# Layer 3 of a recurrent network with experts: two pairs of state space groups written amid the blocks of experts

## The chip, the core and the metric

The kernel runs on one core of one Trainium2 chip. A core has five engines with a queue of instructions each: TensorE (PE, with its weight loads PEld), VectorE (DVE), ScalarE (ACT), GpSimd (POOL) and SyncE (SP). The metric is the device time of one execution in microseconds, as the median of several runs.

## What is computed

The program is four layers over an input of 2 sequences of 1024 tokens with 128 features. Each layer has the form

```
xn = layernorm(x)
s = sequence_mixer(xn)          # layer 3: two state space models, forward and backward
g = silu(mixture_of_experts(xn))
x = x + s * g
```

Only layer 3, the last, matters here. Its mixer runs one state space model over the first 64 features and one, backwards in time, over the other 64; both end in a common projection. Cut to one direction:

```
zxbcdt = u @ in_w.T                       # split into z, x, B, C, dt
x, B, C = silu(conv(x, B, C))             # 4 taps along time
h = exp(dt * A) * h + dt * outer(x, B)    # the state, step by step
y = (h @ C + D * x) * silu(z)
out = rmsnorm(y) @ outp_w.T
```

Its mixture sends each token to 2 of 16 experts and adds a shared expert:

```
hidden = silu(x @ gate[e]) * (x @ up[e])
out = sum over the token's two experts of weight * (hidden @ down[e]) + shared(x)
```

## The kernel before

**State space.** The 2048 tokens are 16 tiles of 128, in four groups (g = 0 to 3) of four tiles. The class `StateSpace` (L413) handles a unit of one direction, one sequence b and one half n of it, that is one group of tokens. `pairs` in `layer3` (L1659) lists four pairs of units, forward and backward together: pair 0 is the first half of sequence 0 in each direction's own sense, pair 1 its second half, pairs 2 and 3 the same for sequence 1. The backward direction starts at the end of its sequence, so pair 3 ends the groups 2 and 3. A pair has two steps:

- `stacked` (L452) makes convolved inputs: the products `px` (L287, the helper that records every matmul) and Silu into `uxs` (L473), and the gates `pz` into `usz` (L483).
- `unit` (L535) does the rest. `uda` (L556) and the product `pd` and Exp into `uE` (L559) make decays inside a tile of 128 tokens; `uwide` (L562) and `pe` make `ueA` (L568); transposes `pt` (L578) make `uxdt` (L580), `uxst` (L581) and `uBt` (L583); `pcb` and `ucb` (L589) are multiplied into `uE` (L592); `pst` and `ustate` (L612) carry the state from tile to tile; `py` (L627) and `pi` (L635 to L637) make the output `uy`; its squares `ut` (L638) are summed by `pss` into `ur` (L299 to L301, with a square root on ScalarE between two VectorE instructions), and `pyo` is scaled by `ur` and added into `xn` (L1736).

`unit` takes `busy`: when it is true, `uda`, `uwide`, `uxst`, the multiplication into `uE` and the two last steps of `uy` are VectorE's, else GpSimd's. Pairs 0, 1 and 2 have it true, pair 3 false. `together` (L654) steps its generators in turn, so that a pair's directions, and the `stacked` of the next pair, are written interleaved. All of `StateSpace` takes its PSUM banks from a pool of four, the experts from another of four.

**Experts.** `Dispatch` (L1129) sorts the tokens by expert into 47 lists of 128 rows. They are worked in twelve blocks of four (three in the last). A block gathers its rows by indirect DMAs on GpSimd's queue (`load`, L1231, `xb`, two buffers), loads weights on SP's queue (`weights`, L1237, `tw`, three buffers), and on TensorE does transposes `pxb` (L1772), the product `pgb`, transposes `phb` (L1784) and the product `pob`; ScalarE has the Silu `sgb` (L1779), VectorE the product `hb` (L1781), and copies `xbT`, `hbT`, `yb` go to VectorE and ScalarE in turn (`Kern.copy`, L278 to L284). Each list's result is scattered into `ys` by an indirect DMA on GpSimd's queue (`store`, L1241). The shared expert (`pgt`, `put`, `hT` L1804, `psh`) is written behind the blocks into `acc`.

**The end.** For each group `fetch` (L1246) loads its slots `yt` from `ys` on SP's queue (L1252, four buffers), which waits for every scatter, and VectorE adds them to `acc` (L409). Then come a Silu (L1813), the product with `xn`, which holds the state space's result (L1814), the sum with x (L1815) and the output's DMA (L1816).

**Order.** The source is written in this order: `stacked` for pairs 0 and 1, the unit pair 0, all blocks of experts, the shared expert, pairs 1, 2 and 3, the fetches. Instructions don't run in the written order: in the build (L1864, `schedule_with_timeline_sim=True`) a scheduler that models time places them in each engine's queue, and the written order is its priority. On the chip each queue then runs strictly in the built order. Layer 2's attention alone has an order written by hand.

Of the kernel before, what the change touches and what calls it, by code (L numbers as in the profile page):

```python
# [653 lines left out]
def together(*parts):  # L654

    live = list(parts)
    while live:
        live = [p for p in live if next(p, p) is not p]


def grp(a, g):
    return a[:, g * G : (g + 1) * G, :]
# [996 lines left out]
def layer3(K, x, xn, xT, w, inp, out):  # L1659
    nc, tc, c = K.nc, K.tc, K.c  # L1660
    four = [P, G, P]
    with ExitStack() as es:
# [84 lines left out]
        space = StateSpace(K, pa, sa, parts)  # L1747
        pairs = [[(m, b, n) for m in parts] for b in range(NB) for n in range(TPB // G)]
# [6 lines left out]
        def load_rows(n0):  # L1755
            loaded[n0] = pf.tile(four, F32, name="xb", bufs=2)
            for n in range(n0, min(n0 + 4, d.n)):
                d.load(loaded[n0][:, n - n0, :], n)

        load_rows(0)  # L1760
        for n0 in range(0, d.n, 4):
            part = range(n0, min(n0 + 4, d.n))
            m = len(part)
            if n0 + 4 < d.n:
                load_rows(n0 + 4)
            xb = loaded.pop(n0)
            tw = pf.tile([P, 4, 256], F32, name="tw", bufs=3)
            for n in part:
                d.weights(tw[:, n - n0, :], n, inp["rows"])
            pt = sf.tile(four, F32, name="pxb", tag="ps")[:, :m, :]  # L1770
            for r in range(m):
                nc.tensor.transpose(pt[:, r, :], xb[:, r, :], c["ident"])  # L1772
            xbT = pf.tile(four, F32, name="xbT", bufs=2)[:, :m, :]
            K.copy(xbT, pt)
            pg = sf.tile(four, F32, name="pgb", tag="ps")[:, :m, :]
            for r in range(m):
                K.mm(pg[:, r, :], xbT[:, r, :], tw[:, r, :P])
            sg = pf.tile([P, 4, 64], F32, name="sgb", bufs=2)[:, :m, :]
            nc.scalar.activation(sg, pg[:, :, :64], AF.Silu)  # L1779
            hb = pf.tile([P, 4, 64], F32, name="hb", bufs=2)[:, :m, :]  # L1780
            nc.vector.tensor_mul(hb, sg, pg[:, :, 64:])  # L1781
            pt = sf.tile([64, 4, P], F32, name="phb", tag="ps")[:, :m, :]
            for r in range(m):
                nc.tensor.transpose(pt[:, r, :], hb[:, r, :], c["ident"])  # L1784
            hbT = pf.tile([64, 4, P], F32, name="hbT", bufs=2)[:, :m, :]
            K.copy(hbT, pt)
            po = sf.tile(four, F32, name="pob", tag="ps")[:, :m, :]
            for r in range(m):
                K.mm(po[:, r, :], hbT[:, r, :], tw[:64, r, P:])
            yb = pf.tile(four, F32, name="yb", bufs=2)[:, :m, :]  # L1790
            K.copy(yb, po)
            for r, n in enumerate(part):
                d.store(yb[:, r, :], n)
        acc = pa.tile([P, NT, P], F32, name="acc", tag="acc")
        for g in range(NG):
# [10 lines left out]
            for j in range(G):  # L1806
                K.mm(po[:, j, :], hT[:, j * P : (j + 1) * P], w["sd"])
            K.copy(grp(acc, g), po)
        for n, p in enumerate(pairs[1:]):
            together(*(space.unit(*u, busy=n < 2) for u in p), *(space.stacked(q) for q in pairs[n + 2 : n + 3]))  # L1810
        for g in range(NG):
            d.fetch(pe, acc, g, w12)
            nc.scalar.activation(grp(acc, g), grp(acc, g), AF.Silu)  # L1813
# [5 lines left out]
def build(tc, io, packs):  # L1819
    nc = tc.nc  # L1820
    with ExitStack() as ctx:
        pool = ctx.enter_context(tc.tile_pool(name="const", bufs=1))
        x = pool.tile([P, NT, P], F32, name="x")
        src = io["x"].rearrange("b (t p) d -> p (b t) d", p=P)
        for g in range(NG):
            nc.sync.dma_start(grp(x, g), src[:, g * G : (g + 1) * G, :])
        xn = pool.tile([P, NT, P], F32, name="xn")
        xT = pool.tile([P, T], F32, name="xT")

        def load(into, n, by=nc.scalar):  # L1830
            t = into.tile([P, packs[n].n], F32, name="w_" + n)
            by.dma_start(t, io[n])
            return View(t, packs[n])

        K = Kern(tc, load(pool, "c"))
        dram = ctx.enter_context(tc.tile_pool(name="lists", bufs=1, space=DRAM))
        lists = {n: dram.tile([rows, P], F32, name=n) for n, rows in (("xs", T), ("ys", 2 * T))}
        views = {}
        with tc.tile_pool(name="const0", bufs=1) as pool0:
            w0 = load(pool0, "l0")  # L1840
            e0 = load(pool0, "e0")
            layer0(K, x, xn, xT, w0, e0)
        later = ctx.enter_context(tc.tile_pool(name="const3", bufs=1))
        views["l3"] = load(later, "l3")
        pair = lists["xs"], lists["ys"]
        with tc.tile_pool(name="const2", bufs=1) as pool0:
            views.update((n, load(pool0, n)) for n in ("l1", "l2"))
            layer1(K, x, xn, xT, views["l1"], {"rows": io["rows1"], "lists": pair, **{n: io[n] for n in ("sw1", "sw3", "sw2")}})
            layer2(K, x, xn, xT, views["l2"], {"rows": io["rows2"], "lists": pair})
        layer3(K, x, xn, xT, views["l3"], {"load": lambda pool: load(pool, "x3", nc.sync), "rows": io["rows3"], "lists": pair}, io["out"].rearrange("b (t p) d -> p (b t) d", p=P))  # L1850
# [17 lines left out]
```

## Time and profile before

| what | us |
|---|---|
| runs | 1360.89, 1365.46, 1372.87 |
| median | 1365.46 |
| the profiled execution, its own time | 1410.96 |
| its span from the first to the last instruction | 1409.1 |
| TensorE busy in the span | 1153.0 |
| VectorE busy | 877.0 |
| ScalarE busy | 623.3 |
| GpSimd busy | 430.2 |

The profiled execution took 45.5 us longer than the median of the runs; its granted TensorE clock was 0.883 on the mean. Positions in the profile are in us from the span's start. Layer 3 begins near 1117, its first gather of rows is issued at 1188.6. In a line of the timeline stand start, duration, engine, source line, operation, out<-in, shape and count, and in brackets the idle time of the engine ahead of it and what ended it. In the chain of waits stand start, duration, engine and what. A float32 matmul shows as two records in the timeline.

### The profile page before, as it was taken

To read this page: it belongs to the slowest core of one execution; us is meant where nothing else is said; L and a number is where in the kernel's file an instruction comes from. 1 tells how busy PE (TensorE), PEld (TensorE's weight loads), DVE (VectorE), ACT (ScalarE), POOL (GpSimd) and SP (SyncE) were. 2 spreads that over 40 slices of the span, in tenths; PEclk is the share of its full clock that TensorE was granted. 3 is DMA by queue.
4 is the path that set the end of the run, shared out by engine and by line. 5 is a ranking of instruction groups with operands and counts; after the bars stand their busy time and mean duration, and the time that the engine had idled before them with its cause. 6 is when DMAs were issued, how large, how long until landed. Compare 5 with 4: busy or idle time off the path is not lost. (4 is left out here: it accounts for less than half of the span.)

```text
span 1409.1 us, 19118 instructions
## 1 busy us (share of the span) xinstructions
PE 1153.0 (82%) x6813; PEld 800.4 (57%) x6813; DVE 877.0 (62%) x2169; ACT 623.3 (44%) x1042; POOL 430.2 (31%) x424
## 2 busy tenths in 40 slices
PE   5599776797997568999998997599998379788885
PEld 2276455785897335444444433377787355657664
DVE  6536336945654776777777635977673577544356
ACT  7656916116322251554556674125522164253351
POOL 0352260036455240000000000156565122556543
PEclk9799986889999876899999898899999768897897
DMA  2000003113343200000000000133345311222311
GB/s 87 0 1 1 0 15 119 46 41 123 119 143 102 60 1 0 1 1 1 1 1 16 8 1 8 75 86 116 120 135 161 104 37 56 66 67 80 53 44 52
DMA packets 49040, 75.71 MB, mean 54 GB/s; under 512 B 7336, under 2 KB 36403, under 8 KB 48689
## 3 DMA queue, kind: packets, MB, share of 16 engines
q1 hardware_dynamic: 39632, 54.30, 12.3%
q0 software_dynamic: 8448, 14.98, 4.7%
q10 hardware_dynamic: 864, 5.21, 1.0%
q8 instruction: 54, 0.88, 0.3%
q14 instruction: 42, 0.34, 0.1%
HBM read 63.95 MB, written 12.85 MB: 55 GB/s over the span
## 5 line engine op out<-in xcount | busy, mean ns | idle before, releaser
L1458 DVE TENSOR_REDUCE mx<-pm 128x1 f32<-128x512 f32 (+3 forms) x304 | 182.0, 656 | 65.3 <-PE pm L287 63.0
L1231 POOL DMA_INDIRECT xb<-xs,dfrom x132 | 134.9, 1022 | 158.3 <-PE pxb L1772 35.4
L1502 ACT ACTIVATE pr<-psc 128x1024 f32<-128x1024 f32 x144 | 139.5, 1021 | 95.1 <-PE psc L287 61.4
L1241 POOL DMA_INDIRECT ys<-yb,dto x132 | 134.5, 1019 | 87.7 <-DVE yb L1119 34.7
L1206 POOL TENSOR_TENSOR dhh<-dhh,w_c 128x1280 fp32r<-128x1280 f32 (+2 forms) x3 | 8.8, 2917 | 476.0 <-DVE dhh L1205 476.0
L287 PE MATMUL pm<-kT,qT 32*128 32x128 f32 (+3 forms) x576 | 118.8, 365 | 16.4 <-DVE mx L1458 12.5
L287 PE MATMUL p<-xbT,tw 128*128 128x256 f32 x368 | 103.0, 396 | 8.4 <-ACT sg L1112 3.0
L287 PEld LDWEIGHTS pm<-kT,qT 32*128 32x128 f32 x576 | 69.1, 203 | 68.9 <-DVE mx L1458 49.1
L1112 ACT ACTIVATE sg<-p,tw 128x256 f32<-128x256 f32 x92 | 41.1, 473 | 102.4 <-PE p L287 86.5
L287 PE MATMUL pat<-pr,va 128*32 128x512 f32 x576 | 82.0, 637 | 0.2 <-ACT pr L1502 0.2
L293 PE MATMUL tp<-w_c,xn 128*128 128x128 f32 x64 | 20.2, 428 | 71.8 <-DVE xn L328 44.0
L287 PEld LDWEIGHTS p<-xbT,tw 128*128 128x128 f32 x368 | 63.8, 196 | 20.3 <-issue 5.8
L1113 DVE SCALAR_TENSOR_TENSOR hh<-p,tw,sg 128x256 f32<-128x256 f32 x92 | 42.6, 478 | 44.2 <-ACT sg L1112 22.9
L287 PE MATMUL psc<-qT,kT 32*128 32x512 f32 x288 | 64.1, 490 | 3.3 <-ACT pr L1502 3.1
L287 PEld LDWEIGHTS po<-tw,hh 128*128 128x128 f32 x368 | 54.2, 192 | 8.7 <-issue 2.2
L293 PEld LDWEIGHTS tp<-w_c,xn 128*128 128x128 f32 x64 | 11.8, 190 | 80.3 <-DVE xn L328 28.1
L287 PE MATMUL po<-tw,hh 128*128 128x128 f32 x368 | 56.2, 276 | 1.0 <-DVE hh L1113 0.7
L287 PE MATMUL psc<-mT,onesR 32*128 32x512 f32 x288 | 53.8, 414 | 0.0
L282 ACT COPY xbT<-pxb 128x256 f32<-128x256 f32 (+3 forms) x39 | 15.6, 400 | 70.8 <-PE pxb L808 35.4
L287 PEld LDWEIGHTS psc<-qT,kT 32*128 32x128 f32 x288 | 30.3, 189 | 16.5 <-ACT pr L1502 14.4
L287 PE MATMUL pd<-uda,w_c 128*128 128x512 f32 x64 | 38.1, 708 | 0.9 <-ACT usz L528 0.9
L287 PE MATMUL pcum<-kv,w_c 128*128 128x512 f32 x64 | 34.2, 635 | 3.4 <-DVE prod L1322 3.1
(528 smaller groups left out, 2824.5 us busy)
## 6 DMA issues: line engine op xcount, KB each, us to landing
tw<-in_rows SPq DMA_DIRECT2D x23, 836.0 KB
tw<-in_rows SPq DMA_DIRECT2D x39, 384.0 KB
yt<-ys SPq DMA_DIRECT2D x24, 256.0 KB
tw<-in_rows SPq DMA_DIRECT2D x47, 128.0 KB
xb<-xs,dfrom POOLq DMA_INDIRECT x132
ys<-yb,dto POOLq DMA_INDIRECT x132
xs<-xn SPq DMA_DIRECT2D x8, 256.0 KB
w_l<-in_l ACTq DMA_DIRECT2D x1, 1890.0 KB
```

The source lines that it names most:

```text
L282: self.nc.scalar.copy(out, in_)
L287: self.nc.tensor.matmul(out, lhsT=lhsT, rhs=rhs, start=start, stop=stop)
L293: self.nc.tensor.transpose(pt[:, j, :], src(g * G + j), self.c["ident"])
L1112: nc.scalar.activation(sg, p1[:, k - k0, :], AF.Silu, bias=t[:, 1536 + k : 1537 + k])
L1113: nc.vector.scalar_tensor_tensor(hh[:, k, :], p2[:, k - k0, :], t[:, 1540 + k : 1541 + k], sg, ALU.add, ALU.mult)
L1206: nc.gpsimd.tensor_mul(h, h.bitcast(F32), c["slot"][:, at].unsqueeze(2).to_broadcast(shape))
L1231: self.K.nc.gpsimd.indirect_dma_start(dst, None, self.xs, bass.IndirectOffsetOnAxis(self.of_token[:, n : n + 1], 0))
L1241: d = self.K.nc.gpsimd.indirect_dma_start(self.ys, bass.IndirectOffsetOnAxis(self.to[:, n : n + 1], 0), src, None, bounds_check=2 * T - 1, ...
L1458: nc.vector.tensor_reduce(mx[:, starts.index(a), g, j : j + k], tile[0][:, : k * m].rearrange("p (j m) -> p j m", m=m), AX.X, ALU.max)
L1502: K.nc.scalar.activation(pr, ps, AF.Exp, scale=scale)
```

## The change

In `layer3` pairs 1 and 2 are written ahead of blocks 5 and 9 (the loop's n0 = 16 and 32), each with the `stacked` of the pair behind it; pair 3 stays behind the shared expert. Which pairs are `busy` stays the same.

```diff
+        def pair(n):
+            together(*(space.unit(*u, busy=n < 3) for u in pairs[n]), *(space.stacked(q) for q in pairs[n + 1 : n + 2]))
+
         load_rows(0)
         for n0 in range(0, d.n, 4):
+            if n0 in (16, 32):
+                pair(n0 // 16)
             part = range(n0, min(n0 + 4, d.n))
...
             K.copy(grp(acc, g), po)
-        for n, p in enumerate(pairs[1:]):
-            together(*(space.unit(*u, busy=n < 2) for u in p), *(space.stacked(q) for q in pairs[n + 2 : n + 3]))
+        pair(3)
         for g in range(NG):
             d.fetch(pe, acc, g, w12)
```

## The prediction

> **What bounds the kernel now.** I read the busy time by stage of layer 3, then the chain that ended last, then the queues of GpSimd and TensorE. Below, "pair k" is the k-th of the four pairs of state space groups (0 to 3), "block k" the k-th of the twelve blocks of experts. The change touches pairs 1, 2 and 3.
>
> ```profile
> core 0: us, PE busy (x) PEld busy (x) DVE busy (x) ACT busy (x) POOL busy (x), PEclk, DMA share, GB/s
> 1231.00:1295.40 64.40, 55.66 (x287) 40.45 (x286) 27.45 (x63) 25.04 (x38) 37.40 (x37) 0.83 0.25 69
> 1295.40:1350.30 54.90, 47.61 (x261) 33.66 (x261) 22.95 (x53) 23.43 (x36) 29.86 (x30) 0.88 0.32 52
> 1350.30:1363.90 13.60, 10.81 (x41) 5.96 (x40) 4.21 (x12) 6.43 (x11) 9.09 (x9) 0.87 0.02 2
> 1363.90:1390.00 26.10, 22.11 (x152) 17.52 (x150) 22.36 (x59) 11.86 (x17) 8.58 (x7) 0.93 0.35 102
> 1390.00:1409.00 19.00, 7.20 (x32) 6.90 (x32) 6.76 (x19) 3.15 (x6) 4.92 (x4) 0.59 0.09 28
> ```
>
> The cuts are the ends of pairs 0, 1 and 2 and of the last scatter. TensorE is 87% busy under pairs 1 and 2 and sets the pace there. So pairs 1 and 2 already run amid the blocks: pair 2's last product (pyo) ends at 1350.3, block 12's product (pob) at 1359.4. The scheduler of the build made that order, though the source writes them behind the blocks. What lies behind the last scatter is pair 3, and the last 19 us are nearly empty.
>
> ```profile
> 1362.89 2.21 DMA ys<-yb,dto
> 1365.26 0.38 SPq L1252
> 1365.69 4.37 DMA yt<-ys
> ...
> 1390.81 2.48 POOL uy L636 x2
> 1393.29 1.23 POOL uy L637
> 1394.54 0.64 ACT ut L638
> 1395.22 3.57 PE pss L287 x16
> 1398.80 1.93 PE pyo L287 x8
> ```
>
> This is the chain: block 12's last scatter, the fetch of all slots that must wait for it, VectorE's sums, then the tail of pair 3 (gates on GpSimd, square, pss, pyo). From the end of the last scatter's issue (1363.9) to the end (1409.1) it is 45.2 us.
>
> ```profile
> 1357.23 0.99 POOL L1241 DMA_INDIRECT ys<-yb,dto  x1 [0.30 <-issue]
> 1358.21 1.08 POOL L556 TENSOR_TENSOR uda<-w_c,vdA 128x512 f32<-128x512 f32 x1
> 1360.27 1.02 POOL L1241 DMA_INDIRECT ys<-yb,dto  x1 [0.98 <-ACT yb L282]
> ...
> 1371.45 2.12 POOL L581 TENSOR_TENSOR uxst<-uxdt,vex 128x512 f32<-128x512 f32 x2 [5.68 <-DVE uxdt L580]
> 1377.44 5.84 POOL L592 TENSOR_TENSOR uE<-uE,ucb 128x512 f32<-128x512 f32 x4 [3.87 <-DVE ucb L589]
> ```
>
> GpSimd issues a gather or scatter every 1.3 us (1.0 and 0.3 between), four per block each way, and does pair 3's elementwise work in the same queue.
>
> **The change part by part.** No operation is added or removed but two ACT table loads; `busy` is true for pairs 1 and 2 and false for 3, as before. Written places only set priorities, so I compared the built orders. They are equal on all engines until block 5 and on SP throughout (no weight load changes its place; block 12's waits for block 9's pob to free its buffer, near 1338, and is first used some 20 us later). Then the state space runs one block ahead of where it ran, and pair 3 is pulled forward. TensorE after pair 2's end, and GpSimd's end, now read:
>
> ```
> PE   pd, phb10, pd x2, pob10, pxb11, pd, pe, pgb11, phb11, pob11, pxb12,
>      pe, pt, pgb12, pt, pcb, phb12, pst x4, pob12, shared ..., py, pi, pss, pyo
> POOL xb12 x3, ys9 x4, uda x2, ys10 x4, uwide, ys11 x4,
>      uxst x2, uE x4, ys12 x3, uy x4
> ```
>
> Before, pair 3's uxst, uE and all its products from the last pd on stood behind block 12's scatters.
>
> *What moves ahead of block 12.* On TensorE one pd (1.0), pe (2.1), pt (2.1), pcb (1.95), four pst (1.2): 8.3 us by the rows behind 1362 in this trace. On GpSimd uxst and uE, 2.1 + 5.8 us. All of it sits on the way to the last scatter, so it is not hidden.
>
> *Delay of the last scatter, D.* Let T0 be the end of block 10's input transposes (pxb), which free block 12's gather. Before, pair 2's second pi ended at 1342.2. One block less now lies ahead of it (0.66 + 1.13 + 0.60 + 1.16 = 3.5), block 9's pob and block 10's pxb follow it (1.8), and TensorE's 15.9 us of waits between 1231 and 1350 (its bracketed idle times in the timeline) shrink a little, since two long ones (before pob and pe) get other work in between; I take 1.5. T0 = 1342.2 - 3.5 + 1.8 - 1.5 = 1339.0. From there the GpSimd queue, in order:
> - gather of block 12, 0.4 + 3.8, then ys9 4 x 1.3: T0 + 9.7 with the gap;
> - uda x2, 2.1: T0 + 11.8. Pair 3's third pd stands behind this on TensorE and waits about 2 us (by durations in order, TensorE is there at T0 + 8.7); behind it wait pob10 and all of block 11;
> - ys10: its product is copied at about T0 + 13.6, so a wait of 1.8, then 5.2: T0 + 18.8; uwide 0.9;
> - ys11: block 11's Silu waits for an exp-to-Silu table load, so yb is ready at about T0 + 21.3; then 5.2: T0 + 26.5;
> - uxst, 2.1: T0 + 28.7. The four pst, and block 12's pob behind them on TensorE, wait for this (2 us);
> - uE x4 at 1.08 (as uxst) to 1.49 (its own median): 4.3 to 6.0, I take 5.0[...]; T0 + 33.7;
> - ys12 3 x 1.3: T0 + 37.5 = 1376.5.
> So D = 1376.5 - 1363.9 = 12.6 us. Lower end: no waits in the queue (33.7) and all 15.9 us of TensorE's waits gone: D near -6. Upper end: below, under the slower rival.
>
> *Tail, S.* Counted from the end of the last scatter's issue, by the rows of before: first yt used at +4.3, the second at +6.3 (1368.2 and 1370.15); twelve adds at 0.3 to +9.9; hT 0.7; copy 0.7; two multiplications and two additions to x 3.4; eight adds 2.2: +16.9. Pair 3's py and pi run under ys12 and its uy right behind (5.0); its squares queue on ACT behind group 0's Silu (to +10.9), pss and pyo 3.6 + 3.7 at the low clock of the old tail: +18.2. But its Sqrt stands on ACT behind group 2's Silu: 16.9 + 0.8 + table 1.3 + 0.4 = +19.4, so this decides. Then eight xn 2.2 and recip 0.2: +21.8; the rest of group 3 with group 2's close 3.8; Silu 0.8; multiply and add 1.4; the output 3.5 as before: +31.3. Tail 31.3 against 45.2: S = 13.9.
>
> Sum: 12.6 - 13.9 = -1.3 us, 1409.1 to 1407.8. The profiled execution took 1410.96, the median of the runs is 1365.46 (a factor of 0.968), so -1.3 there too: about 1364.
>
> [...] First the table loads. Row: ACT_TABLE_LOAD 1.28 us, the activation behind it starting at once (1303.45 + 1.28, then 1304.74). [...] Two loads more and one on the tail's path: by the row +1.3 on the path (in S already)[...]. Second, GpSimd for elementwise work. Rows: uE takes 0.684 us on VectorE and 1.49 on GpSimd. [...] here it is nearer 2.2 times. This speaks against the change: before, these six operations delayed no scatter; now they cost 7.1 us ahead of the last one. [...]
>
> **Rivals.**
> (1) *Traded, my forecast*: scatter later by about as much as the tail shortens; its own range is 1356 to 1372. For it: TensorE at 87% has no room for pair 3 for nothing.
> (2) *GpSimd and the waits don't bind*: most of the 15.9 us of waits are filled and D is 0 or less. Then S remains: -13.9, 1351.5. For it: TensorE was idle 2.8 us of the 13.6 between 1350.3 and 1363.9. Against it: the pulled-forward products need GpSimd results behind scatters.
> (3) *Slower: GpSimd's queue becomes the bound.* Place: uda behind ys9, and uxst behind ys11, each holding TensorE, whose blocked pob holds the next scatter. Price: if each round trip costs the longest wait of GpSimd for TensorE in before (7.0, instead of the 2 I took) that is +10; uE at its largest 1.71 adds 1.8[...], so about +12, and 1377; with a third such trip at ys10 about +17, 1382. It decides once the last scatter is issued later than 1363.9 + 13.9 = 1377.8, only 1.3 us behind my sum, and costs over 1% from 1391.5.
> (4) *It does next to nothing*, since pairs 1 and 2 were amid the blocks already: 1365.5. Against: pair 3 does move.
>
> **Numbers.** About 1% (14 us) is what a measurement can tell from no change. Chances: (1) 0.50; (4) 0.14; (2) 0.18, two thirds of it beyond 1%; (3) 0.18, most of it beyond 1%. Hence faster 0.12, same 0.72, slower 0.16. The range goes from (2) at 1351 to between the two prices of (3), 1379.
>
> **What would show it.** Right: last scatter near 1376; a tail of about 31; uxst and uE directly before block 12's scatters; the 5.3 us hole of TensorE before pss off the chain. Wrong: a last scatter before 1366 (rival 2) or after 1390 (rival 3), or a tail over 38, in which case pair 3's gates, not the fetch, still end last.

## The result, and the profile after

| | median us | lowest to highest | runs |
|---|---|---|---|
| before | 1361.18 | 1355.2 to 1372.87 | 22 |
| after | 1369.96 | 1362.55 to 1374.98 | 22 |

The ratio is 1.0056, with a 95% interval from 1.0041 to 1.0071: 8.8 us more, where the forecast was 1.3 us less. It is a loss of less than 1%, but clear of the noise: the interval is 0.15% to each side, where the prediction took 1% for the least that can be told.

First the busy time by stage of layer 3 in the changed kernel (core 0, span 1368.0 us), cut as in the prediction: pairs 1 and 2, then to the end of the last scatter's issue, then the tail in two pieces. Each row has the window, its length, the busy time and count on TensorE, its weight loads, VectorE, ScalarE and GpSimd, the granted clock and the DMA share.

```profile
core 0: us, PE busy (x) PEld busy (x) DVE busy (x) ACT busy (x) POOL busy (x), PEclk, DMA share, GB/s
1209.00:1258.00 49.00, 45.08 (x263) 33.34 (x262) 25.30 (x57) 23.32 (x34) 32.40 (x31) 0.92 0.30 82
1258.00:1298.70 40.70, 40.54 (x258) 29.73 (x257) 20.62 (x48) 23.91 (x35) 26.44 (x27) 1.00 0.40 69
1298.70:1335.40 36.70, 29.25 (x162) 21.36 (x161) 12.94 (x36) 15.48 (x23) 24.82 (x25) 0.86 0.09 14
1335.40:1349.00 13.60, 7.64 (x48) 5.74 (x48) 10.52 (x23) 3.48 (x6) 4.98 (x4) 0.78 0.50 141
1349.00:1368.00 19.00, 6.37 (x44) 5.15 (x42) 11.93 (x37) 5.31 (x8) 0.00 (x0) 0.77 0.22 65
```

This table must not be set beside the one in the prediction. The chip of that profile is not on record, but its stages are those of a chip on which the kernel takes some 1415 us (the first experiments below give the grounds); this one was taken where it takes 1361. The same rows of the kernel before from a chip of the second kind (run before_third, span 1357.0), for pairs 1 and 2 and the time to the last scatter:

```profile
core 0: us, PE busy (x) PEld busy (x) DVE busy (x) ACT busy (x) POOL busy (x), PEclk, DMA share, GB/s
1208.50:1256.50 48.00, 45.22 (x285) 32.88 (x285) 26.38 (x59) 24.11 (x37) 32.47 (x32) 0.99 0.29 85
1256.50:1299.00 42.50, 41.20 (x261) 30.10 (x260) 23.87 (x56) 23.30 (x36) 33.21 (x33) 1.00 0.40 74
1299.00:1312.40 13.40, 10.61 (x39) 5.67 (x38) 3.54 (x9) 6.29 (x10) 9.03 (x9) 0.87 0.02 3
```

Read it so: in both kernels pairs 1 and 2 take 90 us together (48.00 + 42.50 and 49.00 + 40.70). But before, 13.4 us remain from there to the last scatter, and after 36.7. TensorE is idle for 7.4 of these 36.7 us, and the clock is 0.86.

To compare runs I count from the start of dhh, the last large GpSimd product ahead of layer 3's first gather. "E" is the end of the last scatter's issue, "tail" the rest of the span:

| profile | chip's time of the kernel before | E | tail | stage |
|---|---|---|---|---|
| before, of the prediction | not on record; about 1415 by its stage | 186.7 | 45.2 | 231.9 |
| before_third | 1360 | 148.8 | 44.6 | 193.4 |
| after | 1361 | 171.1 | 32.6 | 203.7 |

So, like for like, the last scatter is 22.3 us later (forecast 12.6) and the tail is 12.0 us shorter (forecast 13.9): 10.3 us longer in these two profiles, 8.8 by the runs.

The GpSimd queue of the changed kernel behind pair 2, from its timeline:

```profile
1303.29 0.98 POOL L1241 DMA_INDIRECT ys<-yb,dto  x1 [0.30 <-issue]
1304.29 2.05 POOL L556 TENSOR_TENSOR uda<-w_c,vdA 128x512 f32<-128x512 f32 x2
1310.42 1.02 POOL L1241 DMA_INDIRECT ys<-yb,dto  x1 [4.09 <-ACT yb L282]
...
1319.87 0.99 POOL L1241 DMA_INDIRECT ys<-yb,dto  x1 [3.94 <-DVE yb L284]
...
1324.68 2.07 POOL L581 TENSOR_TENSOR uxst<-uxdt,vex 128x512 f32<-128x512 f32 x2
1326.69 4.96 POOL L592 TENSOR_TENSOR uE<-uE,ucb 128x512 f32<-128x512 f32 x4
1331.81 1.02 POOL L1241 DMA_INDIRECT ys<-yb,dto  x1 [0.17 <-issue]
```

The order is the forecast one, and uda, uxst and uE take what was put in (2.1, 2.1, 5.0). The two waits in brackets, 4.1 and 3.9 us, are where it runs late. TensorE at the same place, where the four products of pob, two records each, are an x8:

```profile
1305.40 2.08 PE L287 MATMUL pd<-uda,w_c 128*128 128x512 f32 x2 [4.40 <-POOL uda L556]
1307.40 2.07 PE L287 MATMUL pob<-tw,hbT 64*128 64x128 f32 x8
1309.41 1.11 PE L1778 MATMUL pxb<-w_c,xb 128*128 128x128 f32 x4
...
1316.36 0.63 PE L1790 MATMUL phb<-w_c,hb 128*64 128x128 f32 x4 [2.27 <-DVE hb L1787]
```

TensorE waits 4.40 us for uda, and what follows runs at half clock, granted 0.50 from 1305.5 to 1312.2: pob takes 2.07 us where the next one takes 1.16, pxb 1.11 where 0.66 is usual (before_third). Pieces of the chain that ended last, from the last scatter on:

```profile
1334.41 2.08 DMA ys<-yb,dto
1336.65 3.90 DMA yt<-ys
...
1346.37 2.09 PE psh L287 x8
...
1353.77 1.28 ACT L300
1355.06 0.21 ACT ur L300
```

The tail ends by the fetched slots and the table load in front of group 3's Sqrt, no longer by pair 3's gates, as forecast. 32.6 us were measured, 31.3 forecast.

### The profile page after: what moved, and what is told of

Read it like the earlier page. It is cut to its first block, busy times and chain, and to the rows that moved or that the text cites. A ratio compares the mean times of both kernels' runs of the same rounds, so it can differ in the third digit from the quotient of the medians.

```text
span 1368.0 us, 19121 instructions
## 1 busy us (share of the span) xinstructions
PE 1140.1 (83%) x6813; PEld 794.4 (58%) x6813; DVE 876.3 (64%) x2169; ACT 625.0 (46%) x1044; POOL 429.5 (31%) x424
## 3 DMA queue, kind: packets, MB, share of 16 engines
q1 hardware_dynamic: 39632, 54.30, 12.8%
## 5 line engine op out<-in xcount | busy, mean ns | idle before, releaser
L282 ACT COPY xbT<-pxb 128x256 f32<-128x256 f32 (+3 forms) x39 | 15.6, 399 | 66.9 <-PE pxb L808 45.2
## 6 DMA issues: line engine op xcount, KB each, us to landing
w_l<-in_l ACTq DMA_DIRECT2D x1, 1890.0 KB, 11.4
```

The lines of the kernel that those rows point to most:

```text
L282: self.nc.scalar.copy(out, in_)
```

## The experiments

Two explanations stood against each other at the start. **Queue**: the loss is pair 3's uda, uxst and uE between GpSimd's scatters, with TensorE held behind them. **Order**: the loss lies already in pairs 1 and 2, whose shift leaves one more block behind pair 2, whatever pair 3 does. A third came in after the first runs, **chip**: the sum was read off a profile from a chip on which this stage takes another time. In the diffs `decays` puts pair 3's uda and uwide on VectorE, `inside` its uxst and uE.

### Does the profile of before show this kernel, and on which chip?

before_again, before_third and before_fourth are the kernel before, unchanged; after_again and after_third the changed one, unchanged.

before_again, as expected on record:

> The kernel before, unchanged, for a second profile. The first profiled execution of it took 1410.96 us, 50 us over the median of the runs, while that of the changed kernel took 1369.84, its median. If the first was an outlier, this one is near 1361 us, with about 196 us from the last multiplication by the slots (uninterrupted start of the dispatch, 1177.2 in the first profile, 232 us before its end) to the end, and a tail behind the last scatter well under 45 us. If profiling simply slows this kernel, it is near 1410 again.

before_third, as expected on record:

> The kernel before, unchanged, for a profile on the chip of this call. Theory C (chips differ): on a chip where before runs near 1361 us, layer 3 from its last one-hot multiplication (dhh) to the end takes about 195 us, with few waits of an engine that no engine ends; on one near 1415 us about 235 us, as in the two profiles had so far.

before_fourth, as expected on record:

> The kernel before, for a profile from the same chip as the other two. About 193 us from dhh to the end and no idle time of VectorE without a shown releaser if the kernel takes about 1360 us here; 232 to 238 us and more than 20 us of such idle time if it takes about 1416.

Measured: before_again took 1418.51 us, on a chip where the median of before over 59 runs was 1417.62. So it is not profiling that slows it, since all 59 runs there took about as long. My expectation of about 1361 missed; the "near 1410" of the other branch came out, but not for the reason that it gives. before_third took 1358.86 (median there 1360.25), before_fourth 1363.22 (1360.75). The runs fell on five chips: two take about 1360 us, three 1414 to 1418, and no median in between occurred. Of the 59.6 us between the spans of before_again and before_third (1416.6 and 1357.0), 44.3 lie in this stage: 237.7 against 193.4 us. There, on the longer chips, VectorE stands idle in pieces of 1.5 to 5.2 us for which the profile shows no releaser. Three of them, from the timeline of before_again, and TensorE's wait behind the first:

```profile
1246.06 0.42 DVE L1781 TENSOR_TENSOR hb<-sgb,pgb 128x256 f32<-128x256 f32 x1 [4.45 <-issue]
1246.54 0.63 PE L1784 MATMUL phb<-w_c,hb 128*64 128x128 f32 x4 [3.02 <-issue]
...
1329.78 0.29 DVE L608 COPY ustate<-pst 128x128 f32<-128x128 f32 x1 [2.47 <-remote]
...
1341.60 0.75 DVE L627 SCALAR_TENSOR_TENSOR uy<-uxs,w_l,py 128x512 f32<-128x512 f32 x1 [3.80 <-remote]
```

In the stage such pieces of over 1 us make 28.6 us on VectorE in before_again, and none in before_third. In the profile of the prediction they make 25.0, and its stage takes 231.9 us; this is why I count it among the longer chips. TensorE's bracketed waits between the ends of pairs 0 and 2 tell them apart as well: 15.9 us in the profile of the prediction and 16.0 in before_again, but 4.0 in before_third and in before_fourth. What makes the idle pieces was not found.

after_again, as expected on record:

> The changed kernel, unchanged, beside the variants of this call on the same chip. If the loss is in the order of the instructions and not in the chip: 1.004 to 1.007.

after_third, as expected on record:

> The changed kernel unchanged. On a chip where the kernel before takes about 1416 us: by the theory that the forecast's sum holds on the chip whose profile it was read from, the last scatter is issued 12 to 13 us later after dhh than in the kernel before (about 199 against 187), the tail is 32 to 33 against 45.2, and the ratio is 0.999 to 1.002. By the rival (the change costs the same everywhere) the ratio is 1.005 to 1.007 and the last scatter 20 us or more later. On a chip where the kernel before takes about 1360 us it only repeats: 1.0055 to 1.0065.

Both fell on chips of 1360 us: 1.0065 [1.0041, 1.0089] and 1.0074 [1.0045, 1.0103]. E is 171.0 and the tail 32.7 in each, the same picture as in the first profile of the changed kernel. The changed kernel without any edit was not run on a chip of 1415 us; the filled variants below stand in for it.

### Pair 3's decays off GpSimd

```diff
-            pool.tensor_mul(da, ...)
+            made.tensor_mul(da, ...)      # made: VectorE for pair 3, too
-        pool.tensor_copy(wide, ...)
+        made.tensor_copy(wide, ...)
```

after_decays, as expected on record:

> The changed kernel with pair 3's uda and uwide on VectorE; uxst, uE and the gates of uy stay on GpSimd. Theory Q (GpSimd's queue): the 4.4 us wait of TensorE for uda, which stood behind block 9's scatters, goes; ratio 1.0056 - 4.4/1361 = 1.002. With it and the whole set on VectorE having been 0.9984, this and the run with uxst and uE moved (1.0041) share the 0.007 between them. Theory P (TensorE's order): 1.0056.

before_decays, as expected on record:

> The kernel before with pair 3's uda and uwide on VectorE instead of GpSimd: the control for the same edit in the changed kernel, which brought 1.0065 down to 1.001. If that gain was the removal of a wait that only the changed kernel has (uda behind ys9, with TensorE held at pd), the kernel before gains little from the same edit: 0.998 to 1.000. If it is merely VectorE's being quicker at these tiles, the kernel before gains as much, 0.5%: 0.995.

after_decays took 1361.71 us, ratio 1.0010 [0.9989, 1.0030], on the chip where after_again gave 1.0065. The edit was thus worth about 0.55%, 7.7 us. But the profiles show that most of this is not the wait for uda. E is 168.5 us, only 2.5 earlier than in after_again and 19.6 later than in before_third; the tail is 26.9 us instead of 32.7, so 5.8 shorter. The control fell on a chip of 1415 us and gave 0.9965 [0.9938, 0.9992], although its TensorE does not wait for uda at this place: its E of 188.0 lies between the 186.7 and 192.5 of the kernel before, and its tail is shorter by the same 5.8 us (39.4 against 45.2).

The edit also does more than it says. It moves pair 3 in the built order, in both kernels. In after_decays the first half of pair 3's gates on GpSimd stands ahead of block 12's scatters and holds them by 2.5 us (their yb is ready at 1327.8):

```profile
1326.64 0.98 POOL L1243 DMA_INDIRECT ys<-yb,dto  x1 [0.30 <-issue]
1327.64 2.50 POOL L638 TENSOR_TENSOR uy<-uy,ut 128x512 f32<-128x512 f32 x2
1330.31 1.00 POOL L1243 DMA_INDIRECT ys<-yb,dto  x1 [0.17 <-issue]
```

And TensorE still waits 2.4 us for uda, now made on VectorE. So the run takes 2.5 us from the delay of the last scatter, perhaps 5 without those gates (an estimate: 2.5 + 2.5), and the rest of its gain is a shorter tail, which the kernel before gets from the same edit.

### Pair 3's products held behind the last block

```diff
-        pair(3)
+        with tc.issue_after(latest.ins):   # latest: the last block's last product, pob
+            pair(3)
```

after_p3behind, as expected on record:

> The changed kernel with all of pair 3's TensorE work held behind the product of the last block; the order up to pair 2's end stays that of the changed kernel. If the pull of pair 3 ahead of the last blocks is what costs: last scatter about 15 us earlier than in the changed kernel, tail longer by 10 to 12, ratio 1.002 or 1.003. If the first half costs (the blocks one behind the state space from block 5 on): the same 1.0056 or more.

Measured 1381.27 us, 1.0155 [1.0129, 1.0181], far from the 1.002 to 1.003 that Queue gave. The whole time is no fair test, since the edit holds back more than the kernel before does, in which three of pair 3's four pd run well ahead of the last scatter. The last scatter is one: if the loss were pair 3 between the scatters alone, taking it out would have brought E back to 148.8. From GpSimd's timeline of this run, where nothing of pair 3 stands between the scatters, and then from TensorE's:

```profile
1304.67 0.98 POOL L1241 DMA_INDIRECT ys<-yb,dto  x1 [2.16 <-ACT yb L282]
...
1314.78 0.98 POOL L1241 DMA_INDIRECT ys<-yb,dto  x1 [5.27 <-DVE yb L284]
```

```profile
1305.60 2.05 PE L287 MATMUL pgb<-tw,xbT 128*128 128x128 f32 x8 [0.83 <-issue]
...
1311.70 2.07 PE L287 MATMUL pob<-tw,hbT 64*128 64x128 f32 x8 [0.72 <-ACT hbT L282]
```

GpSimd waits about as long as with pair 3 in its queue. E is 162.7 after dhh, 13.9 later than in before_third, with no pair 3 ahead of it; the tail is 53.1. The last three blocks end their pob 7 to 12 us apart (128.9, 141.2, 151.2, 158.3 with the one before them): a chain of gather, transposes, products and copies, in which TensorE has little else to do (16.2 us idle up to E, against 9.0 in before_third). It also runs partly at half clock: the granted clock is 0.56 from 1298.6 to 1312.6 and 0.74 from there to 1334.6, and pob takes 2.07 us at 1301.7 and again at 1311.7, where 1.16 was its time at 1290.3. By the durations of its products some 6 us of the chain are that, an estimate. This speaks for Order, with the clock as a part of it that was not tested by itself. Pair 3 in these holes costs 8.3 us at E (171.0) and saves 20.4 in the tail (32.7), against holding all of it back: pulling pair 3 forward pays; it mends part of what the order of pairs 1 and 2 cost.

### Pair 3's elementwise work on VectorE

```diff
-            together(*(space.unit(*u, busy=n < 3) for u in pairs[n]), ...)
+            together(*(space.unit(*u, busy=n < 3, inside=n == 3) for u in pairs[n]), ...)   # after_inside
+            together(*(space.unit(*u, busy=True) for u in pairs[n]), ...)                   # the allvec runs
```

after_inside, as expected on record:

> The changed kernel with pair 3's uxst and uE on VectorE instead of GpSimd; TensorE's order stays the same but for one product, uda, uwide and the gates of uy stay on GpSimd. Theory Q (GpSimd's queue: pair 3's elementwise work ahead of the last scatters is what the change costs): the last block's scatters start when its yb is ready, 2.6 us earlier than in the changed kernel's profile (1329.2 instead of 1331.8), ratio to before about 1.0037 instead of 1.0056. Theory P (TensorE's order: the blocks fall one behind and pair 3's products stand ahead of the last block): no change, 1.0056.

after_allvec, as expected on record:

> The changed kernel with all of pair 3's elementwise work on VectorE, so that GpSimd issues gathers and scatters only. Theory Q: the 4.4 us wait of TensorE for uda and the 2.6 us of the last scatters go, 7 us together, ratio about 1.0005; the last scatter is issued about 7 us earlier. Theory P: the order on TensorE still puts pair 3 ahead of the last block, ratio 1.003 to 1.008.

before_allvec, as expected on record:

> The control: the kernel before with all of pair 3's elementwise work on VectorE. It tells how much of a gain of the one above is only that VectorE is faster for the same work. Both theories: pair 3's uE takes 0.68 instead of 1.49 us and the gates 0.6 instead of 1.24, at the end of the chain, 2 to 5 us less, ratio 0.997 to 0.999. If pair 3's tail is not what ends last in an undisturbed run, 1.000.

after_allvec2, as expected on record:

> The changed kernel with all of pair 3's elementwise work on VectorE (busy true for all), again, on a chip where the kernel before takes about 1360 if the chip is such a one. On the chip of 1417 us it was 0.998. Theory GpSimd's queue (the loss on the quick chip is mostly pair 3's uda, uxst and uE standing between scatters): 0.994 to 1.000, at most as slow as with the decays alone (1.001). Rival (the order of pairs 1 and 2 loses 5 to 9 us by itself, whichever engine does pair 3's work): 1.000 to 1.004.

before_allvec2, as expected on record:

> The kernel before with all of pair 3's elementwise work on VectorE. It tells whether the written place of the pairs brings anything once GpSimd has only gathers and scatters: if pulling pair 3 forward shortens the tail by more than it delays the scatters, this is slower than the changed kernel with the same edit; if the order of pairs 1 and 2 is the loss, this is quicker, 0.990 to 0.997, and the quickest of the four.

All five fell on chips of 1415 us.

| run | ratio to before on its chip | 95% interval |
|---|---|---|
| after_inside | 1.0041 | 1.0016 to 1.0067 |
| after_allvec | 0.9984 | 0.9955 to 1.0014 |
| before_allvec | 0.9986 | 0.9957 to 1.0014 |
| after_allvec2 | 0.9978 | 0.9951 to 1.0004 |
| before_allvec2 | 0.9964 | 0.9940 to 0.9988 |

The changed kernel without an edit was not run on such a chip, so whether moving uxst and uE alone helps it stays open, and the expectations, made for chips of 1360 us, decide nothing here between Queue and Order. With all of it on VectorE both kernels lie a little under before, clear of the noise only in before_allvec2, and the written place of the pairs makes no difference that these intervals tell. By the profiles the change trades here too: E is 206.3 and 200.6 us with it, 181.5 and 191.0 without, the tail 28.2 and 26.2 with it, 37.5 in both without. The best of all runs are before_allvec2 and before_decays, 0.36 and 0.35% under before; neither has the change in it, and neither was run on a chip of 1360 us.

### The half clock where pair 1 ends

On the chips of 1360 us TensorE's clock halves where pair 1 ends, in the changed kernel only. From the busy time by stage, first after_third (its pair 1 ends in this window), then before_fourth for the same 9 us after dhh:

```profile
core 0: us, PE busy (x) PEld busy (x) DVE busy (x) ACT busy (x) POOL busy (x), PEclk, DMA share, GB/s
1249.48:1258.48 9.00, 9.00 (x48) 8.52 (x48) 3.62 (x13) 2.25 (x5) 6.84 (x7) 0.62 0.40 105
```

```profile
core 0: us, PE busy (x) PEld busy (x) DVE busy (x) ACT busy (x) POOL busy (x), PEclk, DMA share, GB/s
1253.73:1262.73 9.00, 8.91 (x62) 7.29 (x62) 5.76 (x18) 5.76 (x10) 6.87 (x7) 1.00 0.39 118
```

In the first profile of the changed kernel the granted clock is 1.00 from 1209.9 to 1250.7, 0.50 from 1250.9 to 1257.6 and 1.00 again from 1257.7 to 1305.3; a mean of 0.62 over 9 us, at half or full clock, is the same 6.8 us at half. TensorE is busy nearly all the time in both, but does 48 records in the one and 62 in the other. Just ahead of it the changed kernel waits 1.42 us for hb and 0.64 for ut; at this place before_third has one wait, of 0.96. First after_again, then before_third:

```profile
1249.54 0.63 PE L1790 MATMUL phb<-w_c,hb 128*64 128x128 f32 x4 [1.42 <-DVE hb L1787]
1250.80 1.05 PE L287 MATMUL pss<-w_c,ut 128*128 128x1 f32 x8 [0.64 <-ACT ut L638]
```

```profile
1249.37 1.13 PE L287 MATMUL pgb<-tw,xbT 128*128 128x128 f32 x8 [0.96 <-ACT yb L282]
```

The runs fill the first wait, in the block at n0 = 20, with transposes (after_fill, after_fill2) or true products (the others) of a constant, whose result is overwritten by the block's own:

```diff
+            for r in range(10 if n0 == 20 else 0):     # after_fill, after_fill2
+                nc.tensor.transpose(pt[:, r % 4 % m, :], c["ident"][:, :64], c["ident"])
+            for r in range(6 if n0 == 20 else 0):      # after_fillmm, after_fillmm_b; 9 in after_fillmm9
+                K.mm(pt[:, r % 4, :], c["ident"][:, :64], c["ident"])
             for r in range(m):
                 nc.tensor.transpose(pt[:, r, :], hb[:, r, :], c["ident"])
```

after_fill, as expected on record:

> The changed kernel with ten transposes of a constant (128x64 to 64x128, about 0.15 us each, 1.5 us together) put on TensorE between pgb and phb of one block, where pair 1 ends and TensorE waits 1.42 us for hb; everything else keeps its place in the built order. The fillers' result is overwritten by the block's own transposes. Theory clock (the wait of 2 us for hb and ut is what brings the 6.8 us at half clock that follow, and these are the 5 us by which pair 2 ends later than my sum): the granted clock of the stretch behind stays near 1.00 instead of 0.62, pob, pxb, pss and pyo there take 1.16, 0.66, 0.95 and 1.14 us as in the kernel before, pair 1 ends some 3 us earlier after dhh, and the last scatter is issued 2 to 4 us earlier (about 168 us after dhh instead of 171): ratio 1.003 to 1.005 to the kernel before. Rival (the half clock comes from something else, or what is won there is waited away at uda in pair 3): clock or time unchanged, ratio 1.006 to 1.007.

after_fill2, as expected on record:

> The changed kernel with ten transposes of a constant on TensorE in the wait for hb where pair 1 ends. On a chip where the kernel before takes about 1360 us: theory clock: the half clock of 6.8 us behind it is gone (1.00 granted), the last scatter 2 to 4 us earlier than in the changed kernel (167 to 169 after dhh, not 171): ratio 1.003 to 1.005. Rival: 1.006 to 1.007. On a chip of about 1416 us, where the waits lie elsewhere, it equals the changed kernel beside it within 0.2%.

after_fillmm, as expected on record:

> As after_fill, but the filler in the wait for hb is six true matmuls of constants (64x128 out, about 0.26 us each, 1.5 us together) in place of the ten transposes. With the transposes TensorE was busy 5.03 us of the 6 ahead of the half-clock period, as in the kernel before, and yet the period came. Theory [...]: on a chip of about 1360 us the period of 6.8 us is gone or put off, pob, pxb, pss and pyo behind it take 1.16, 0.66, 0.95 and 1.14 us, and pair 1 ends 3 us earlier after dhh (90.5, not 93.6); pair 2 too (131.5, not 134.4) if TensorE's work is the bound there. Rival (the period has another cause, the remaining wait for ut of 0.6 us or one set by the time alone): clock 0.62 and pair 1's end at 93.6 again. On a chip of about 1416 us it shows only whether the clock of this stretch changes.

after_fillmm_b, as expected on record:

> The changed kernel with six matmuls of constants (1.5 us) in the wait for hb where pair 1 ends, once more. On a chip where the kernel before takes about 1360 us: [...] the half clock of 6.8 us behind pair 1 is gone, pair 1 ends at 90.5 after dhh and pair 2 at 131.5, and the ratio falls from 1.0065 to 1.003 to 1.005; if the period has another cause, clock 0.62, pair 1's end 93.6 and pair 2's 134.4 again, ratio 1.006 to 1.008.

after_fillmm9, as expected on record:

> The same with nine matmuls (2.3 us): longer than the wait, so hb's transposes come 0.6 to 0.8 us later, and with hardly any idle time before them. If the clock is held up by it and not by six, [...] pair 1 ends 2 to 3 us earlier than 93.6. If neither holds it, the idle time ahead of the period is not its cause, and this one is 0.6 us slower than six.

Only after_fill2 fell on a chip of 1360 us: 1.0076 [1.0048, 1.0104], no gain. In the 6 us ahead TensorE was then busy for 5.03 us, as in before_fourth (5.04), and yet the clock behind it was 0.62 again, and pair 1, pair 2 and E ended where they did (93.6, 134.4, 171.0):

```profile
core 0: us, PE busy (x) PEld busy (x) DVE busy (x) ACT busy (x) POOL busy (x), PEclk, DMA share, GB/s
1243.42:1249.42 6.00, 5.03 (x45) 4.44 (x41) 5.32 (x9) 2.04 (x4) 4.66 (x4) 1.00 0.34 103
1249.42:1258.42 9.00, 9.00 (x47) 8.52 (x47) 3.62 (x13) 2.25 (x5) 6.86 (x7) 0.62 0.39 105
```

So that wait, filled with transposes, is not what decides the clock. Whether true products in the same place would have changed it was not shown, since the runs with them fell on the other kind of chip: after_fillmm 1.0017 [0.9995, 1.0039], after_fillmm_b 1.0025 [0.9993, 1.0056], after_fillmm9 1.0052 [1.0027, 1.0077]. The last one is 5.9 us longer than after_fillmm by the medians, though three products add only 0.7 us of TensorE's time (2.18 for nine, 1.52 for six); with nine the built order of GpSimd, ScalarE and VectorE changes as well, which it does not with six products or ten transposes. What sets off the half clock stays open.

These runs show another thing. On chips of 1415 us the changed kernel with a harmless filler is at 1.0018 [0.9983, 1.0053] (after_fill), 1.0017 and 1.0025, on a chip of 1360 with the same filler at 1.0076. This points to a change that costs less, or nothing, on the kind of chip from which the forecast was read, and 0.6 to 0.8% on the other; "points to" is all that may be said, since the kernel without filler was not run there. The intervals of after_fillmm and after_fill2 do not touch; those of the same kernel, after_fill and after_fill2, overlap by 0.0005.

## Why the prediction was wrong

**"-1.3 there too".** This is the step that failed first: a sum of two large terms of opposite sign, 12.6 and 13.9, was carried from one chip to another because the two times stand at 0.968. They are not scaled copies. The 59.6 us between two such spans lie for the most part in the very stage that the change touches. On the chips of 1415 us the two terms are about right: E, by the forecast 199.3 after dhh, is 198.8 to 201.9 in the three filled variants (after_fill and the two with six products) against 186.7 and 192.5 in two profiles of the kernel before, so 6 to 15 us later (forecast 12.6), with a tail of 32.4 against 45.2, so 12.8 shorter (forecast 13.9). Their small sum is not settled there: the two profiles of the kernel before differ by more, and with a filler the ratios are 1.0017 to 1.0025, where the forecast was 0.9991. On the chips of 1360 us the first term is 22.3. That the profiled execution stood 45.5 us above the median was in my text, and should have been a warning that the profile might be of another machine.

**T0, "1342.2 - 3.5 + 1.8 - 1.5".** By this formula and before_third's second pi of pair 2 (127.45 after dhh) block 10's pxb should end at 124.2; it ends at 129.5, 5.3 us later. The block less ahead of pair 2 has saved nothing: pair 2's second pi ends at 127.8, against 127.45. What failed here is the waits. I had counted 1.5 us from "TensorE's 15.9 us of waits", which were to shrink. On this chip TensorE's waits from the end of pair 0 to that pi are 3.0 us in before_third and 3.8 in the changed kernel: there was little to fill, and they grew by 0.8. Another 3.1 us is the half clock behind pair 1, which the sum does not have, by durations in after_again and before_third: pob 1.67 instead of 1.16, pxb 1.11 instead of 0.66, four products of pss 1.71 instead of 0.95, the two pyo 3.77 instead of 2.36. Together these make 5.4 us, which covers the 5.3. In the profile of the prediction the clock under pairs 1 and 2 was 0.83 and 0.88, in before_third 0.99 and 1.00, so here there was a full clock to lose. That the 3.1 us would come back with a full clock is argued, not shown.

**uda behind ys9, "waits about 2 us".** GpSimd was nearly on time: uda began at T0 + 10.5 (forecast 9.7). TensorE was early, at T0 + 7.2 and not 8.7, and waited 4.40 us for the first of the two. Then pd, pob and pxb ran at half clock, so the next scatters began at T0 + 16.6 and not 13.6, and block 11's at + 26.1 and not 21.3. E is T0 + 41.6 (forecast 37.5). after_decays bears on this step and gives it less than its ratio of 1.0010 suggests: with uda off GpSimd's queue E is 2.5 us earlier, and the other 5.8 are a shorter tail. after_p3behind sets the limit: with nothing of pair 3 in the queue E is still at T0 + 33.2. That this is near the "33.7" of my lower end is chance, since it is reached without pair 3; the three blocks left behind pair 2 take it by their own chain, in part at half clock.

So of the 9.7 us by which the last scatter's delay was missed, 5.3 are T0, 4.1 the queue behind it, and 0.3 that before_third itself goes from pair 2's pi to E in 21.35 us instead of 21.7. My rival (3), at 0.18, was the nearest: slower, with uda's round trip as its place. But half of the miss lay ahead of that place, at T0, and uxst, its second place, cost little: the last block's yb was ready at 1329.2, and its scatters started at 1331.8, only 2.6 us later.

**The tail** was right in mechanism and near in size, 32.6 for 31.3; the fetch's first use came at + 5.2 instead of + 4.3. The table load took 1.28 us and the Sqrt began 0.01 us later, as in the row that I took. uE took 4.96 us for four, my 5.0, which was an estimate. By the medians of one it is 1.286 us on GpSimd against 0.678 on VectorE, 1.9 times, where I had 2.2. In the profile of the prediction the four took 5.84 us, with VectorE busy throughout and a DMA share of 0.30; here VectorE was busy for 3.14 of the 4.96 and the share was 0.01. Which of the two made the difference, if either did, was not tested.

**What the source line decides.** In the built order only the place of pair 1 matters. With pair 1 alone written ahead of block 5, and pairs 2 and 3 behind all blocks, the order on every engine is that of the changed kernel; with pair 1 written one block later, it is that of the kernel before but for 9 of TensorE's 4675 places, 6 of VectorE's 2492 and 3 of ScalarE's 1349. Neither was timed. The change speaks of two pairs; all that it does comes from pair 1's place, with which the scheduler also pulls pair 3 forward. Pair 2's place adds nothing.

## What to carry to other kernels

A profile that stands several per cent off the median of the runs (here 1410.96 against 1365.46 us) may be of another chip, and its waits, the very thing that an edit is to fill, may not exist where the time is measured: ask in which stage the difference lies before a sum of two terms that nearly cancel is scaled across. When independent work is pulled ahead of a pipeline of blocks, ask what the last blocks will overlap with: here they became a chain of steps that wait for each other, 33 us for three blocks and partly at half clock (pob 2.07 us for 1.16), and work put into its holes came at the price of another engine's queue. Where the order is a scheduler's, compare built orders first: they show which part of a change exists at all, and whether an edit meant to move one thing moved others too.

## What the runs showed of the chip

Five chips gave two levels for the same program, medians of 1360.25 and 1360.75 us on two and of 1414.40 to 1417.62 on three; three quarters of the difference between two profiles lies in this one stage, where the longer one has idle pieces of over 1 us for which no releaser is shown: 28.6 us on VectorE, 10.9 on ScalarE, 9.7 on TensorE. The half-clock period behind pair 1 lasts 6.8 us. It came in all six profiles of the changed order at the first level, each time within 0.2 us of the same point after dhh by the durations of pob's products, and in neither profile of the kernel before there. Why it begins at the same instruction in each run, no run here explains.

TensorE's and ScalarE's queues kept their order while the times moved: from 11.4 us after dhh to the end TensorE's 153 groups of records come in one and the same order in the four profiles of the kernel before, though the stage takes 193.4 us in before_third and 237.7 in before_again, and so do ScalarE's 108 in these two.
